# The first steps of a four-layer transformer kernel: extra TensorE products, whole-tile modulations, another order of small work on VectorE, ScalarE and GpSimd

## The chip, the cores and the metric

The kernel runs on one core of a Trainium2 chip. A core has TensorE for products (PE in the profile, and PEld for its weight loads), VectorE (DVE), ScalarE (ACT), GpSimd (POOL) and SyncE (SP), which here issues nearly all transfers. Each engine works through its own instructions in order, and semaphores make it wait for another. The metric is the time of one execution on the device, in microseconds. All data is float32.

## The reference

The input x has 128 sequences of 64 tokens with 128 channels. A condition of 128 vectors and a context of the same shape as x come with it. Four layers follow. The first one is what this case is about:

```python
mod = silu(t_emb) @ adaln_w + adaln_b
sh_sa, sc_sa, g_sa, sh_ff, sc_ff, g_ff = split(mod[:, None, :], 6)
xm = _ln(x) * (1.0 + sc_sa) + sh_sa
qkv = xm @ qkv_w + qkv_b                 # 16 heads of 8 channels
x = x + g_sa * (_attend(q, k, v) @ sa_proj_w + sa_proj_b)
x = x + _attend(_ln(x) @ q_w + q_b, context @ kv_w + kv_b) @ ca_proj_w + ca_proj_b
xm = _ln(x) * (1.0 + sc_ff) + sh_ff
x = x + g_ff * (gelu(xm @ fc1_w + fc1_b) @ fc2_w + fc2_b)
```

Layer 1 is one cross attention, layer 2 has the form of layer 0, and layer 3 is a mixture of three experts with a gate.

## The kernel before

The 8192 tokens are cut into 16 tiles of 512 tokens (8 sequences). A tile of x, `x[s]`, stays in SBUF for the whole program as four blocks of 128 tokens by 128 channels. Layer 0's self attention runs over the 16 tiles, then its cross attention, then its MLP, and so on through the layers.

For one tile of attention, `prepare` is a generator that is advanced piece by piece:

1. statistics: four `bn_stats` and four `bn_aggr` on DVE (L312, L314), then `rs`, the inverse standard deviation, on POOL (L321, L322);
2. `normed_by_pool`: `nmu` (L361) and four `xn` instructions (L364), on POOL, for the very first tile on DVE;
3. four transposes on PE into PSUM (`psT`, L334) and the modulation into `xm`: eight ACT instructions, one per sequence (L351), for the first tile eight on DVE (L349);
4. keys: the product `pk` (L428), the copy `kT` on ACT (L430), and four masked copies `kbd` (L436) on POOL, for the first tile on DVE;
5. queries: `pq` (L441) and `qT` on ACT (L443);
6. values: 32 small products `pvv` (L451) and two ACT copies into `vbd` (L456, L457). There are two `vbd` buffers, and each has to be cleared once by `clear` on POOL (L171 to L173) before its first use.

The attention itself advances in half steps of 256 tokens. `scores` does the score products `sc` (L470), the row maxima `mx` (L477) and the subtraction `e` (L479) on DVE. `turned` transposes `e` on PE (`pp`, L495) and takes exp on ACT (`eT`, L499), and `weighted` multiplies with the values (`po`, L512) and copies out on ACT (`o`, L520). There is only one PSUM buffer for `sc`, so the score products of a step wait for `e` of the step before. All the other products of a half step take turns in two PSUM buffers called `mm`.

In one half step `k` the order on the engines is written out by hand: scores of `k`, first half of the turning of `k-1`, values of `k-2`, a piece of some tile's preparation, the second half of the turning, more pieces of preparation. Before step 0 the pieces are advanced by calls of `ahead_1`; each number is the tile whose `prepare` goes one piece further. `condition` turns the condition and the bias vectors (`pc`, `pv`), and `first_mods` are three parts of the modulation vectors of layer 0 (`pm` on PE, L195, and two additions on DVE, L199). `first_tables` has five parts: the folded bias column (`pb`, L207), the gate table in two halves (`pg`, L224, the copy `gate_rows`, L225, and its transfer), and the folded bias row in two halves (L233, and `pb` with an addition, L237 and L238).

The order is final: the program runs under a manual schedule, and nothing moves instructions later.

Of the kernel before, what the change touches and what calls it, by code (L numbers as in the profile page):

```python
# [9 lines left out]
F32 = mybir.dt.float32  # L10
AF = mybir.ActivationFunctionType
ALU = mybir.AluOpType
# [3 lines left out]
P = 128  # L16
NST = 16
TT = 4
NB = 8
L = 64  # L20
# [39 lines left out]
def tile_kernel(ctx: ExitStack, tc: tile.TileContext, a: dict, out: bass.AP):  # L60
    nc = tc.nc
    V, S, G, T = nc.vector, nc.scalar, nc.gpsimd, nc.tensor
# [3 lines left out]
    def const(shape, name):  # L66
        return cp.tile(shape, F32, tag=name, name=name)
# [4 lines left out]
    out_d = out.rearrange("b n c -> (b n) c").rearrange("(s t p) c -> s p t c", t=TT, p=P)  # L72


    cond = const([P, P], "cond")
    nc.sync.dma_start(cond, a["cond_1024"])
    vec_rows = const([_NVEC, P], "vec_rows")
# [13 lines left out]
                nc.sync.dma_start(t, src.rearrange("(k p) n -> p k n", p=P))  # L91
                w[name] = t

    xs = [const([P, TT, P], f"x{s}") for s in range(NST)]

    def load_groups(which):
        for s in which:
            nc.sync.dma_start(xs[s], x_d[s])

    load_groups((0,))  # L100
    load_weights(("L0_xcond_adaln", "L0_xcond_qkv"))
    load_groups((1,))
    load_weights("L0_xcond_sa")
# [3 lines left out]
    for name, n in (("L0_xcond_ca_proj_b", P), ("L1_xcond_bp", P), ("L2_xcond_b_cproj", P), ("L3_xcond_router_b", 3)):  # L107
        t = const([P, n], name)
# [11 lines left out]
    make_identity(nc, ident)  # L120
    nhalf = const([P, TT], "nhalf")
    G.memset(nhalf, -0.5)

    stack, attention_stack = ExitStack(), ExitStack()
    dp = ctx.enter_context(tc.tile_pool(name="dp", bufs=1, space=bass.MemoryType.DRAM))
# [34 lines left out]

    def mm(name):
        return pools[1].tile([P, 512], F32, tag="mm", name=name)

# [4 lines left out]
    def clear(t):  # L170
        G.memset(t, 0.0)  # L171
        G.memset(t[0:L, :, :, 16:17], 1.0)
        G.memset(t[L:P, :, :, 17:18], 1.0)  # L173
# [4 lines left out]
    condT = const([P, P], "condT")  # L178
# [64 lines left out]
    def condition():  # L243
        pc = mm("pc")
        T.transpose(pc[:, :P], cond, ident)
        V.tensor_copy(condT, pc[:, :P])
        S.activation(scT, pc[:, :P], AF.Silu)
        pv = mm("pv")
        T.transpose(pv[:, :_NVEC], vec_rows, ident[:_NVEC, :_NVEC])
        V.tensor_copy(vec, pv[:, :_NVEC])  # L250
        V.tensor_scalar_add(vec1, vec, 1.0)
# [43 lines left out]
    def mod(name, i, s):  # L295

        return mods[name][:, i, ts(s, NB)].unsqueeze(2).broadcast_to([P, NB, L])

    def by_batch(t):
        return t.rearrange("p (b l) -> p b l", b=NB)  # L300
# [29 lines left out]
    def transposed(psum, src):  # L330

        ps = psum.tile([P, 512], F32, tag="mm", name="psT")
        for t in range(TT):
            T.transpose(ps[:, ts(t, P)], src[:, t, :], ident)  # L334
        return ps

    def modulated(pool, ps, name, scale, shift, s, tag="xm"):
        xm = pool.tile([P, NT], F32, tag=tag, name=tag)
        V.tensor_tensor(by_batch(xm), by_batch(ps), mod(name, scale, s), ALU.mult)
        G.tensor_tensor(by_batch(xm), by_batch(xm), mod(name, shift, s), ALU.add)  # L340
        return xm

    def modulated_by_batch(pool, ps, name, scale, shift, s, tag="xm", by_dve=False):
        xm = pool.tile([P, NT], F32, tag=tag, name=tag)
        for b in range(NB):
            k = NB * s + b
            m, p = (mods[name][:, i, k : k + 1] for i in (scale, shift))
            if by_dve:
                V.tensor_scalar(xm[:, ts(b, L)], ps[:, ts(b, L)], m, p, ALU.mult, ALU.add)  # L349
            else:  # L350
                S.activation(xm[:, ts(b, L)], ps[:, ts(b, L)], AF.Identity, bias=p, scale=m)  # L351
        return xm


# [2 lines left out]


    def normed_by_pool(pool, src, mv, rs, tag, engine=G):
        nmu = pool.tile([P, TT], F32, tag="nmu" + tag, name="nmu")  # L360
        G.tensor_scalar(nmu, mv[:, :, 0], -1.0, 0.0, ALU.mult, ALU.add)  # L361
        xn = pool.tile([P, TT, P], F32, tag=tag, name=tag)
        for t in range(TT):
            engine.tensor_scalar(  # L364
                xn[:, t, :], src[:, t, :], nmu[:, t : t + 1], rs[:, t : t + 1], ALU.add, ALU.mult
            )
        return xn
# [10 lines left out]
    def prepare(pools, at):  # L378

        pool, psum = pools[:2]  # L380
        s, layer = at["s"], at["layer"]
        eps = 1e-5 if layer == "L1c" else 1e-6
        cross = layer[2] == "c"
        if cross:
            c = pool.tile([P, TT, P], F32, tag="c", name="c", bufs=3)
            nc.sync.dma_start(c, ctx_d[s])
        yield
        if layer == "L1c":
            mv = x_mv[:, s]
            rs = inv_std(pool, mv, eps)  # L390
        else:
            mv, rs = stats_of(pool, xs[s], eps)
        yield
        xn = normed_by_pool(pool, xs[s], mv, rs, "xn", V if at.get("first") else G)
        if cross:
            cn = c
            if layer != "L0c":
                cn = pool.tile([P, TT, P], F32, tag="cn", name="cn", bufs=1)
                for t in range(TT):
                    rs, nb = (v[eps][:, s, t : t + 1] for v in (ctx_rs, ctx_nb))  # L400

                    if layer == "L1c" or s == 0:
                        G.tensor_scalar(cn[:, t, :], c[:, t, :], rs, nb, ALU.mult, ALU.add)
                    else:
                        S.activation(cn[:, t, :], c[:, t, :], AF.Identity, bias=nb, scale=rs)
        yield
        if layer == "L1c":
            kv_in = modulated_by_batch(pool, transposed(psum, cn), "L1_xcond_Wss_kv", 0, 1, s, "cm")
        elif cross:
            kv_in = copied(pool, transposed(psum, cn), "cm")  # L410
            if layer == "L0c":
                nc.sync.dma_start(ctxT[s], kv_in)
        else:
            q_in = kv_in = modulated_by_batch(
                pool, transposed(psum, xn), at["wmod"], 1, 0, s, by_dve=at.get("first", False)
            )
        yield
        if not cross:
            pass
        elif layer == "L1c":  # L420
            q_in = modulated(pool, transposed(psum, xn), "L1_xcond_Wss_q", 0, 1, s)
        else:
            q_in = copied(pool, transposed(psum, xn), "xm")
        yield


        pk = psum.tile([P, 512], F32, tag="mm", name="pk")
        T.matmul(pk, at["wk"], kv_in, start=True, stop=True)  # L428
        kT = pool.tile([P, NT], F32, tag="kT", name="kT")
        S.activation(kT, pk, AF.Identity, bias=at["bk"])  # L430
        i = turn[0] % 2
        turn[0] += 1
        vbd = vbds[i]
        kbd = pool.tile([P, 4, NB, L], F32, tag="kbd", name="kbd")
        for j in range(4):
            (V if at.get("first") else G).tensor_scalar(  # L436
                kbd[:, j], by_batch(kT), mask[:, j : j + 1], 1.0, ALU.mult, ALU.mult
            )
        yield
        pq = psum.tile([P, 512], F32, tag="mm", name="pq")  # L440
        T.matmul(pq, at["wq"], q_in, start=True, stop=True)  # L441
        qT = pool.tile([P, NT], F32, tag="qT", name="qT")
        S.activation(qT, pq, AF.Identity, bias=at["bq"])  # L443
        at.update(qT=qT, kbd=kbd)
        yield

        wv_pair = at["wv"].rearrange("p (i j d) -> p j i d", j=2, d=HD)
        pvv = psum.tile([P, NB, L], F32, tag="mm", name="pvv")
        for b in range(NB):
            for j in range(2):  # L450
                T.matmul(  # L451
                    pvv[ts(j, L), b, :], kv_in[:, ts(b, L)], wv_pair[:, j],
                    start=True, stop=True,
                )
        pv4 = pvv.rearrange("p b (i d) -> p b i d", d=HD)
        S.copy(vbd[0:L, :, :, 0:HD], pv4[0:L])  # L456
        S.copy(vbd[L:P, :, :, HD : 2 * HD], pv4[L:P])  # L457
        at["vbd"] = vbd
# [713 lines left out]

    def stages():
        ats = [attention_of(s, layer) for layer in ("L0s", "L0c") for s in groups]
        ats[0]["first"] = True
        ahead_1, steps_1 = attend(pools, ats)
        ahead_2, steps_2 = attend(
            pools, [attention_of(s, layer) for layer in ("L1c", "L2s", "L2c") for s in groups]
# [33 lines left out]
            return turns[last - 1 :]  # L1212


        clear(vbds[0])
        ahead_1(0, 1, 2, 3)
        condition()
        ahead_1(0, 0)
        first_mods[0]()
        ahead_1(0, 0, 1, 2, 0, 0, 1)  # L1220
        psum_for_attention()

        steps_1[0]([lambda: ahead_1(2), lambda: clear(vbds[1]), lambda: ahead_1(1, 1, 0, 3)])
        tables = first_tables()
        steps_1[1]()
        first_mods[1]()
        steps_1[2]()
        for f in tables[:3]:
            f()
        steps_1[3]((), tables[3:])  # L1230
        for f in steps_1[4:6]:
            f()
        first_mods[2]()
        n = last + 2 + len(heads_0)
        for f in steps_1[6:-n]:
            f()
        rest = into_mlp(steps_1, heads_0, turns_0)
        second = [(0, 1, 2), (0,), (1, 0), (0, 0, 1, 2), (0, 1, 1, 2, 0, 0, 3, 3)]
        n_ = len(second)
# [66 lines left out]
```

## Time and profile before

| | |
|---|---|
| median of 3 runs | 1635.25 us (1635.12 to 1635.38) |
| the profiled execution | 1632.74 us |
| its span, first to last instruction | 1631.0 us |
| PE busy | 1577.1 us, 97% |
| DVE busy | 1296.5 us, 79% |
| ACT busy | 1037.2 us, 64% |
| POOL busy | 1084.7 us, 67% |

The busy time is that of one profiled execution. A matmul's end is modelled, so a PE that is busy is not a PE at its peak. One float32 product of `pk` shows as two PE rows. Times in the text such as "at 20.45" are microseconds from the first instruction of the span.

### The profile page before, as it was taken

How to read it: one execution, taken by the hardware profiler on the slowest of the kernel's cores; microseconds unless marked ns; L12 is line 12 of the kernel's file. 1: busy time of each engine (PE TensorE's matmuls, PEld its weight loads, DVE VectorE, ACT ScalarE, POOL GpSimd, SP SyncE). 2: the span in 40 equal slices, each digit the busy share in tenths (PEclk: the TensorE clock that was granted, in tenths of full speed). 3: DMA queues.
4: the chain of work that ended last, by engine and by line, in shares of the span. 5: the costliest groups of instructions: out<-in, count | busy, mean ns of one | idle time of the engine just before them, and what ended most of it. 6: DMA issues, size and time to landing. Idle time of an engine off the chain costs nothing.

```text
span 1631.0 us, 64964 instructions
## 1 busy us (share of the span) xinstructions
PE 1577.1 (97%) x27842; PEld 1089.0 (67%) x27842; DVE 1296.5 (79%) x2430; ACT 1037.2 (64%) x1710; POOL 1084.7 (67%) x1818
## 2 busy tenths in 40 slices
PE   6999999998999899999999999998999999999998
PEld 4677777776554477777777677776777666666665
DVE  7999999998576688899999999997454576666666
ACT  5788777776333587788888888886334544444443
POOL 6688776776799888986778876665876333333322
PEclk9999999999999999999999999999999999999999
DMA  7334443322202022211333532222433111111100
GB/s 208 82 82 97 108 121 91 89 80 62 61 27 59 27 58 62 63 47 49 85 94 82 116 95 63 73 57 57 120 91 78 30 39 37 40 33 35 34 11 20
DMA packets 146783, 112.71 MB, mean 69 GB/s; under 512 B 36357, under 2 KB 125247, under 8 KB 146495
## 3 DMA queue, kind: packets, MB, share of 16 engines
q1 hardware_dynamic: 146288, 108.53, 25.8%
q8 instruction: 219, 3.59, 1.0%
q14 instruction: 69, 0.57, 0.1%
q10 hardware_dynamic: 207, 0.03, 0.0%
HBM read 83.99 MB, written 14.02 MB: 60 GB/s over the span
## 4 chain that ended last, share of the span: by engine, by line
PE 79%; DVE 13%; ACT 3%; POOL 3%; issue 1%; DMA 0%; SPq 0%; POOLq 0%; DVEq 0%; ACTq 0%
PE sc L470 10%; PE pp L495 9%; PE po L512 7%; PE ph L1063 6%; PE ph L1064 6%; DVE e L479 6%; DVE mx L477 6%; PE ph L676 6%; PE po L1094 5%; PE psT L334 5%; PE pk L428 5%; PE py L555 4%; PE py L692 3%; PE pvv L451 3%; PE pq L441 3%; PE py L682 2%
## 5 line engine op out<-in xcount | busy, mean ns | idle before, releaser
L499 ACT ACTIVATE eT<-pp 128x1024 f32<-128x1024 f32 x320 | 329.8, 1030 | 159.4 <-PE pp L495 159.3
L477 DVE TENSOR_REDUCE mx<-sc 128x32 f32<-128x2048 f32 x160 | 366.6, 2291 | 58.6 <-PE sc L470 58.6
L479 DVE TENSOR_TENSOR e<-sc,mx 128x2048 f32<-128x2048 f32 x160 | 366.6, 2291 | 5.4
L495 PEld LDWEIGHTS pp<-ident,e 64*128 64x128 f32 x5120 | 184.9, 139 | 140.7 <-ACT eT L499 44.8
L495 PE MATMUL pp<-ident,e 64*128 64x64 f32 x5120 | 228.7, 229 | 7.1 <-DVE e L479 4.7
L364 POOL TENSOR_SCALAR xn<-x,nmu,rs 128x128 f32<-128x128 f32 x508 | 224.7, 456 | 13.3
L436 POOL TENSOR_SCALAR kbd<-kT,mask 128x512 f32<-128x512 f32 x316 | 213.2, 693 | 26.9 <-ACT kT L430 24.5
L549 POOL TENSOR_TENSOR oT<-o,rb 128x512 f32<-128x512 f32 x80 | 102.3, 1278 | 164.5 <-DMA rb<-recs 63.6
L470 PE MATMUL sc<-kbd,qT 32*64 32x256 f32 x5120 | 180.5, 389 | 16.4 <-DVE e L479 15.4
L677 ACT ACTIVATE h<-ph,vec 128x512 f32<-128x512 f32 x128 | 87.4, 688 | 154.8 <-PE ph L676 154.6
L512 PE MATMUL po<-eT,vbd 128*32 128x64 f32 x10240 | 178.4, 221 | 1.1 <-issue 1.0
L1070 ACT ACTIVATE h<-h 128x512 f32<-128x512 f32 x112 | 70.6, 630 | 148.1 <-DVE h L1066 129.2
L512 PEld LDWEIGHTS po<-eT,vbd 128*32 128x32 f32 x10240 | 151.9, 110 | 14.0 <-issue 1.6
L322 POOL TENSOR_TENSOR rs<-rs,nhalf 128x4 f32<-128x4 f32 x128 | 130.4, 1019 | 10.7
L470 PEld LDWEIGHTS sc<-kbd,qT 32*64 32x64 f32 x5120 | 98.1, 131 | 53.1 <-issue 20.2
L1066 DVE TENSOR_TENSOR h<-ph,ab 128x512 f32<-128x512 f32 x112 | 77.0, 688 | 56.2 <-PE ph L1064 56.1
L312 DVE BATCH_NORM_STATS2 st<-x 128x6 f32<-128x128 f32 x512 | 110.5, 278 | 0.8 <-DMA x<-in_x_dram 0.3
L1099 DVE SCALAR_TENSOR_TENSOR acc<-po,pr,acc 128x128 f32<-128x128 f32 x192 | 67.3, 350 | 44.1 <-PE po L1094 39.5
L1063 PE MATMUL ph<-nx,w 128*128 128x512 f32 x192 | 99.9, 602 | 0.0
L520 ACT COPY o<-po 128x512 f32<-128x512 f32 x160 | 95.8, 598 | 5.2 <-PE po L512 3.6
L1064 PE MATMUL ph<-u,w_ev 128*128 128x512 f32 x192 | 98.0, 592 | 0.0
L1094 PEld LDWEIGHTS po<-w_2o,h 128*128 128x128 f32 x768 | 92.1, 192 | 8.7 <-issue 8.4
(261 smaller groups left out, 2849.8 us busy)
## 6 DMA issues: line engine op xcount, KB each, us to landing
rb<-recs SPq DMA_DIRECT2D x80, 256.0 KB
c<-in_ctx_dram SPq DMA_DIRECT2D x64, 256.0 KB
o<-o SPq DMA_DIRECT2D x320, 32.0 KB
gt<-gate_L_xcond_sa_proj_w SPq DMA_DIRECT2D x32, 256.0 KB
gt<-gate_L_xcond_W_proj SPq DMA_DIRECT2D x32, 256.0 KB
gt<-gate_L_xcond_W_mlp SPq DMA_DIRECT2D x32, 256.0 KB
x<-in_x_dram SPq DMA_DIRECT2D x16, 256.0 KB
ctxT<-cm SPq DMA_DIRECT2D x16, 256.0 KB
```

Of the source, the lines that this page charges most:

```text
L322: G.tensor_tensor(rs, rs, nhalf, ALU.pow)
L364: engine.tensor_scalar(xn[:, t, :], src[:, t, :], nmu[:, t : t + 1], rs[:, t : t + 1], ALU.add, ALU.mult)
L436: (V if at.get("first") else G).tensor_scalar(kbd[:, j], by_batch(kT), mask[:, j : j + 1], 1.0, ALU.mult, ALU.mult)
L470: T.matmul(sc[ts(h, L), g, ts(t2, 256)], qT[ts(g, 32), ts(b, L)], kbd[ts(g, 32), :, b, :], start=True, stop=True,)
L477: V.tensor_reduce(mx, sc.rearrange("p g (m k) -> p (g m) k", k=L), AX.X, ALU.max)
L479: V.tensor_tensor(e, sc.rearrange("p g (m k) -> p (g m) k", k=L), mx.unsqueeze(2).broadcast_to([P, 32, L]), ALU.subtract,)
L495: T.transpose(pp[:, h, ts(4 * g2 + 2 * i + t2, L)], e6[ts(h, L), 2 * gg + g2, t2, i], ident[ts(h, L), ts(h, L)],)
L499: S.activation(eT[:, gg], pp, AF.Exp, scale=HD ** -0.5)
L512: T.matmul(po[ts(g, 32), i, ts(2 * t2 + h, L)], at["vbd"][:, 4 * u + 2 * t2 + h, 2 * g + i, :], e7[:, g // 2, h, g % 2, i, t2, :], start=T ...
L1063: T.matmul(ps, wn, d["nx"], start=True, stop=False)
L1064: T.matmul(ps, we, d["u"], start=False, stop=True)
L1094: T.matmul(po[:, ex, :], d[q][:, ts(t, P)], k3["w_2o"][:, q, :], start=r == 0, stop=r == 1)
```

## The change

All edits concern the first steps.

- A tile `busy` of ones is written by DVE, and `keep_busy(n)` issues n products of it with itself into an `mm` buffer. Nothing reads them. Six stand at the very start of PE's order, three after the first modulation vectors, five after the transposes of tile 0.
- The load of `x[0]` is issued ahead of that of the condition.
- In `condition` the copy `condT` moves from DVE to ACT, behind `scT`, and a small Exp on ACT follows it.
- DVE does the statistics of tile 0 before it copies the bias vectors, and the first modulation vectors before `xn`. `xn` of tile 0 subtracts the mean directly, without `nmu`.
- The modulation of tile 0 is a multiplication and an addition on DVE over the whole 512 tokens. That of tile 2 is a multiplication on DVE and an addition on POOL. Tile 1 and tiles from 3 on stay with eight ACT instructions.
- `clear(vbds[0])` moves behind POOL's work for tile 0's statistics. `clear(vbds[1])` moves behind step 0, which on POOL is behind `kbd` of tile 1, the addition for tile 2 and `xn` of tile 3. DVE's statistics of tile 2 move behind `kbd` of tile 0.
- The second part of the modulation vectors moves from after step 1 to after step 2, and the last part of the tables, the folded row, from step 3 to step 7.

```diff
+    load_groups((0,))
     cond = const([P, P], "cond")
     nc.sync.dma_start(cond, a["cond_1024"])
...
-    load_groups((0,))
     load_weights(("L0_xcond_adaln", "L0_xcond_qkv"))
...
+    taken = const([P, TT], "taken")
+    busy = const([P, P], "busy")
+    V.memset(busy, 1.0)
...
+    def keep_busy(n):
+
+        p = mm("pi")
+        for _ in range(n):
+            T.matmul(p[:, 0:P], busy, busy, start=True, stop=True)
...
-        V.tensor_copy(condT, pc[:, :P])
         S.activation(scT, pc[:, :P], AF.Silu)
+        S.copy(condT, pc[:, :P])
+
+        S.activation(taken, nhalf, AF.Exp)
...
-    def modulated(pool, ps, name, scale, shift, s, tag="xm"):
+    def modulated(pool, ps, name, scale, shift, s, tag="xm", engine=G):
         xm = pool.tile([P, NT], F32, tag=tag, name=tag)
         V.tensor_tensor(by_batch(xm), by_batch(ps), mod(name, scale, s), ALU.mult)
-        G.tensor_tensor(by_batch(xm), by_batch(xm), mod(name, shift, s), ALU.add)
+        engine.tensor_tensor(by_batch(xm), by_batch(xm), mod(name, shift, s), ALU.add)
         return xm
...
     def normed_by_pool(pool, src, mv, rs, tag, engine=G):
+        if engine is V:
+            xn = pool.tile([P, TT, P], F32, tag=tag, name=tag)
+            for t in range(TT):
+                V.tensor_scalar(
+                    xn[:, t, :], src[:, t, :], mv[:, t, 0:1], rs[:, t : t + 1],
+                    ALU.subtract, ALU.mult,
+                )
+            return xn
...
-            q_in = kv_in = modulated_by_batch(
-                pool, transposed(psum, xn), at["wmod"], 1, 0, s, by_dve=at.get("first", False)
-            )
+            first = at.get("first", False)
+            if first or at.get("third", False):
+                q_in = kv_in = modulated(
+                    pool, transposed(psum, xn), at["wmod"], 1, 0, s, engine=V if first else G
+                )
+            else:
+                q_in = kv_in = modulated_by_batch(pool, transposed(psum, xn), at["wmod"], 1, 0, s)
...
-        ats[0]["first"] = True
+        ats[0]["first"] = ats[2]["third"] = True
...
+        keep_busy(6)
+        ahead_1(0, 1, 2, 3, 0)
+        condition()
+        first_mods[0]()
+        keep_busy(3)
+        ahead_1(0)
         clear(vbds[0])
-        ahead_1(0, 1, 2, 3)
-        condition()
-        ahead_1(0, 0)
-        first_mods[0]()
-        ahead_1(0, 0, 1, 2, 0, 0, 1)
+        ahead_1(0)
+        keep_busy(5)
+
+        ahead_1(0, 1, 0, 0, 2, 1)
         psum_for_attention()
 
-        steps_1[0]([lambda: ahead_1(2), lambda: clear(vbds[1]), lambda: ahead_1(1, 1, 0, 3)])
+        steps_1[0]([lambda: ahead_1(2, 1, 1, 0, 3)])
+        clear(vbds[1])
         tables = first_tables()
         steps_1[1]()
+        steps_1[2]()
         first_mods[1]()
-        steps_1[2]()
         for f in tables[:3]:
             f()
-        steps_1[3]((), tables[3:])
+        steps_1[3]((), tables[3:4])
         for f in steps_1[4:6]:
             f()
         first_mods[2]()
         n = last + 2 + len(heads_0)
-        for f in steps_1[6:-n]:
-            f()
+        for k, f in enumerate(steps_1[6:-n]):
+            f((), tables[4:] if k == 1 else ())
```

More of the change, by code (lines that the diff above doesn't have):

```diff
@@ L72, in tile_kernel, with load_groups @@
     out_d = out.rearrange("b n c -> (b n) c").rearrange("(s t p) c -> s p t c", t=TT, p=P)
+    xs = [const([P, TT, P], f"x{s}") for s in range(NST)]
+    def load_groups(which):
+        for s in which:
+            nc.sync.dma_start(xs[s], x_d[s])
+    load_groups((0,))
     cond = const([P, P], "cond")
@@ L92, in load_weights @@
                 w[name] = t
[L94 to L98, printed above, removed]
-    load_groups((0,))
     load_weights(("L0_xcond_adaln", "L0_xcond_qkv"))
@@ L335, in transposed, with modulated_by_batch @@
         return ps
-    def modulated(pool, ps, name, scale, shift, s, tag="xm"):
+    def modulated(pool, ps, name, scale, shift, s, tag="xm", engine=G):
         xm = pool.tile([P, NT], F32, tag=tag, name=tag)
         V.tensor_tensor(by_batch(xm), by_batch(ps), mod(name, scale, s), ALU.mult)
-        G.tensor_tensor(by_batch(xm), by_batch(xm), mod(name, shift, s), ALU.add)
+        engine.tensor_tensor(by_batch(xm), by_batch(xm), mod(name, shift, s), ALU.add)
         return xm
-    def modulated_by_batch(pool, ps, name, scale, shift, s, tag="xm", by_dve=False):
+    def modulated_by_batch(pool, ps, name, scale, shift, s, tag="xm"):
         xm = pool.tile([P, NT], F32, tag=tag, name=tag)
@@ L347, in modulated_by_batch @@
             m, p = (mods[name][:, i, k : k + 1] for i in (scale, shift))
[L348 to L351, printed above, removed]
+            S.activation(xm[:, ts(b, L)], ps[:, ts(b, L)], AF.Identity, bias=p, scale=m)
         return xm
     def normed_by_pool(pool, src, mv, rs, tag, engine=G):
+        if engine is V:
[6 more added lines that the diff above has]
+            return xn
         nmu = pool.tile([P, TT], F32, tag="nmu" + tag, name="nmu")
@@ L363, in normed_by_pool @@
         for t in range(TT):
-            engine.tensor_scalar(
+            G.tensor_scalar(
                 xn[:, t, :], src[:, t, :], nmu[:, t : t + 1], rs[:, t : t + 1], ALU.add, ALU.mult
```

## The prediction

> **What bounds the kernel now.** I read the page's busy rows first, then the table of windows over the first 40 us, then the chain of waits and the timeline there, since every edit lies in the first eight half steps.
>
> ```profile
> PE   6999999998999899999999999998999999999998
> DVE  7999999998576688899999999997454576666666
> 10.00:15.00 5.00, 3.61 (x4) 1.17 (x4) 4.21 (x25) 0.69 (x1) 2.29 (x4) 1.00 0.85 159
> 15.00:20.00 5.00, 2.95 (x68) 2.15 (x68) 3.60 (x5) 2.76 (x9) 4.80 (x12) 1.00 1.21 298
> 25.00:30.00 5.00, 2.92 (x52) 2.74 (x52) 3.97 (x10) 4.29 (x6) 4.73 (x11) 0.83 0.84 255
> 30.00:35.00 5.00, 5.00 (x124) 3.01 (x124) 3.35 (x4) 2.18 (x4) 0.45 (x1) 0.83 0.68 186
> ```
>
> PE is full in nearly every slice but the first (40.8 us, digit 6). The columns of a window are PE, PEld, DVE, ACT, POOL, clock: PE stands still some 2 of 5 us at 15 to 20 and at 25 to 30, and the clock is 0.83 over two stretches, that is half rate for about 3.4 us in all. So the change can win only a few us of 1631.
>
> ```profile
> 9.21 2.12 DVE xm L349 x8
> 11.37 2.09 PE pk L428 x2
> 14.20 1.68 DVE kbd L436 x4
> 17.93 1.11 ACT xm L351 x4
> 24.71 1.28 ACT L499
> 29.21 1.15 PE pm L195 x4
> 30.37 1.83 PE sc L470 x32
> 63.07 2.30 DVE mx L477
> 65.40 2.30 DVE e L479
> ```
>
> The chain passes from one engine to the next until about 40 us, then it settles: sc, mx, e, sc. I call S0, S1, ... the start of the score products (sc) of each half step. The timeline gives 16.02, 22.10, 30.30, 36.90, 43.78, 49.80, 55.95, 61.84, 67.83, 73.77, 79.76. The settled step is 5.97 us (73.77 less 61.84, halved): 1.2 until mx may start, 2.30 mx, 2.30 e, 0.15 to the next sc. Nothing after S0 can go below that, so the whole prize is the shift of S10. The steps of 8.20 (S1 to S2), 6.60 and 6.88 hold 3.8 us of slack; the head holds the rest.
>
> ```profile
> 11.37 2.07 PE L428 MATMUL pk<-xm,L_xcond_qkv_w 128*128 128x512 f32 x2 [2.27 <-DVE xm L349]
> 13.83 0.19 POOL L321 TENSOR_SCALAR rs<-mv 128x4 f32<-128x4 f32 x1
> 15.64 1.87 POOL L364 TENSOR_SCALAR xn<-x,nmu,rs 128x128 f32<-128x128 f32 x4
> 19.45 1.81 POOL L171 MEMSET vbd<- 128x2048 f32 x1
> 20.45 1.12 PE L428 MATMUL pk<-xm,L_xcond_qkv_w 128*128 128x512 f32 x2 [1.49 <-ACT xm L351]
> 29.32 0.58 ACT L456 COPY vbd<-pvv 64x512 f32<-64x512 f32 x1 [0.46 <-PE pvv L451]
> ```
>
> pk takes 2.07 at 11.37 and 1.12 at 20.45: PE is at half rate before its first load (the clock column says 1.00 there, so I go by durations). POOL's rs, xn and memset will matter below.
>
> **The head, S0.** Moving x0 ahead of cond shifts x0 0.45 earlier on SP's queue (stats at 4.15, not 4.60) and cond behind 256 KB. Bounds for cond: 3.5 (its present reach to pc at 3.10, plus one issue) to 4.3 (behind all of x0). I take 4.3; it costs nothing, because pm waits for the adaln weights until 5.71 with the same bytes ahead of them; scT is ready by 5.1 (if cond landed after 4.9, the head would move with it). The fourteen products have no row. Nearest is pm: 1.19 for two products cold, 0.71 at 55.30 warm, so six take 2.1 to 3.6 us from about 1.0 and end by 4.6, under that same wait; three and five take 1.1 to 3.0 in gaps of about 1.2. With a warm clock that is free, and I take warm: PE is busy nearly all of 1.0 to 6.5. condT and the early Exp load (1.28) go to ACT, idle until kT; clear(vbd0), about 2.4 us with its small memsets, sits on POOL in the wait for tile 1's stats: both nothing.
>
> Then: pm 5.7 to 6.4, mods 0.60 to 7.05, xn 1.11 to 8.2 (no nmu, and mods no longer after it), psT to 8.5, xm in two DVE tensor_tensors. Their row is y<-py,gt 128x512 at 0.63 (62.16), so 1.26 in place of 2.11: 9.85. pk 1.06, 0.13 to ACT, kT 0.69, kbd 1.67: 13.5. S0 is 13.6, **2.4 earlier**.
>
> **S1, where it is lost again.** DVE now does tile 2's stats after kbd, but POOL's order still has rs of tile 2 before nmu and xn of tile 1. Stats end at 13.5 + 1.15 = 14.65. In the trace rs started at 13.83 and S1 came 8.27 later through xn, psT, ACT's eight modulations (2.48), pk, psT. All of those stand as they were, so S1 = 14.7 + 8.27 = 23.0, **0.9 later** than before; e of step 0 is done at 19.4 and waits for nobody.
>
> **S2.** Gone: ACT's 2.48 for tile 2 (now 0.63 on DVE inside the sc of step 1, plus an add on POOL), the Exp load, pm (1.22) ahead of S2. With pp, pq, pvv done by S1 + 4.7 the step is DVE's 5.97: 28.95, **1.35 earlier**.
>
> **S3, a new wait.** clear(vbd1) was at 19.45 in idle POOL time. It now stands behind kbd 2.70, the new xm add (1.26, the row of POOL's 128x512 x<-x,gt) and nmu and xn 2.05. From S1 + 0.15 the memset ends at about 31.1. ACT's vbd copies of tile 1 wait for it, and behind them on ACT: eT (free to go at 30.7, goes at 32.3), o, kT; behind those on PE pk, pp, psT, pm, pb. From 32.3: eT 1.02, o 0.59, kT 0.65, then pm 0.7, mods 0.60, pb: S3 = 36.3, **0.6 earlier** only.
>
> **S4 to S10.** pb of the row table (the gap at 43.36 before S4) has left this step: 42.2, 1.55 earlier. gate_rows 0.42 and stats 1.15 now both fall between e and mx: 6.3 for this step, where the trace has 6.02. S5 to S7 go as before, within 0.15. pb (0.25 on PE) and its add (0.29 on DVE) land in step 7, which has 0.3 idle on PE: 0.3 lost. S10 is **0.85 earlier** at full clock. The gate table's DMA leaves 0.5 sooner, the SP queue keeps its order otherwise.
>
> **The clock rule against the trace.** sc in S0 ends at 14.7 and psT of tile 1 comes at 17.0: PE idles 2.3 us. In the trace PE idled 24.86 to 27.07 (2.2 us) and the two 0.83 windows follow, with sc 1.80 in place of 1.12 and pm 1.22 for 0.71. The Trainium skill, "TensorE: Matmul & The Clock Gate", Part 1, wants about 3.4 us of idleness in a free-running window, and its closing table warns only of gaps above 3 us; it gives this gap a price of 0 and the sum -0.85. By the trace a gap of 2.2 us is enough. Price from 0 (half rate over before pk at 21.2) to 1.9 (psT tails 0.3, pk 0.95 and sc 0.68 all slow). I take 0.3: the half-rate stretch of the trace lasted 3.4 us, and from the end of a window near 18 it would be over at about 21.5.
>
> Sum: -0.85 + 0.3 = -0.55. The profiled execution took 1632.74 (span 1631.0 and 1.74 around it), so 1632.2; the runs' median is 2.5 us above it, and I carry that over: 1634.7.
>
> **The rivals.**
> 1. The head start carries to the end. If tile 1 is ready in time (S1 = S0 + 6.08 as before), S1 is 19.7, and S3 and all that follows 3.3 earlier: -4.1, 1631.2. For it: S0 itself is solid. Against: POOL's order, which needs tile 2's stats first.
> 2. Slower, by the clock in the new gap at 14.7. It decides when PE's idle share of a window exceeds what the trace shows to be enough (about 2.2 of 3.4 us); if half rate then lasts past 21.2, the full 1.9 is paid at S1 and S2: +1.05, 1636.3. For it: 2.3 us of idleness. Against: the window must lie right.
> 3. The products do not lift the clock in time. Then pm, psT, pk stay at half rate and the five products delay pk: S0 about 15.2, and S1 moves with kbd: +0.75, 1636.0. Against: PE is busy over any window between 1.0 and 7.8.
>
> **How the numbers follow.** A change of 0.2% (3.3 us) is about what a measurement of this kernel can tell from none. Likeliest case 0.62, own range 1633.6 to 1635.6; rival 1: 0.10, of which 0.08 beyond 0.2%; rival 2: 0.18, rival 3: 0.10, together 0.05 beyond. Range 1632.6 to 1636.9: it leaves out rival 1 and the far ends of the others.
>
> **What would show it.** Right: pk about 1.1 from 9.9; S0 near 13.6; psT of tile 1 not before 16.5; S1 near 23; ACT standing before the vbd copies at 27.7 to 31.1; S10 near 79. Wrong: S1 below 21 (rival 1), clock under 1.00 in 15 to 25 with pk near 2.0 (rival 2), pk above 1.8 (rival 3).

## The result, and the profile after

The changed kernel takes 1637.01 us (median of 22 runs, 1634.81 to 1642.73) beside 1635.14 us for the kernel before on the same chip: ratio 1.0016, 95% interval 1.0010 to 1.0023. Predicted was 1634.7, a little faster; it is a little slower, 0.1 us beyond the upper end of the predicted range, on the side of rival 2. The profiled execution took 1634.81 us (span 1633.0) against 1632.74 (1631.0): 2.0 us more of span, of which 1.7 are there at S10.

The busy rows of the page after: slice 1 of PE is fuller, by the products that nothing reads and by work at half rate; no other digit of PE differs, and none of DVE by more than one tenth.

```profile
PE   7999999998999899999999999998999999999998
DVE  6999999999566688899999999998454576666666
```

The table of windows of the changed kernel (PE, PEld, DVE, ACT, POOL, clock, DMA share, GB/s):

```profile
10.00:15.00 5.00, 3.26 (x15) 1.79 (x13) 4.01 (x14) 1.38 (x2) 1.22 (x2) 1.00 0.89 179
15.00:20.00 5.00, 2.79 (x36) 1.42 (x36) 4.66 (x11) 0.00 (x0) 3.45 (x9) 0.71 1.19 303
20.00:25.00 5.00, 4.34 (x38) 2.95 (x38) 2.15 (x9) 3.72 (x11) 2.79 (x6) 0.50 1.15 287
25.00:30.00 5.00, 4.94 (x72) 2.63 (x72) 3.03 (x3) 2.18 (x3) 4.32 (x8) 0.77 0.90 266
30.00:35.00 5.00, 3.66 (x144) 3.09 (x144) 4.70 (x10) 2.93 (x4) 4.66 (x8) 1.00 0.74 207
```

The clock is 0.71, 0.50 and 0.77 from 15 to 30, where before it was 0.83 twice, later. Its record in the trace gives half rate from 17.1 for 10.2 us; before it was 3.4 us, from 28.3. PE looks busier at 20 to 30 than at 15 to 20, but that is half-rate work. ACT does nothing at all between 15 and 20: it waits for tile 1.

The chain of waits of the changed kernel, in order of time:

```profile
1.76 4.49 DMA L_xcond_adaln_w<-in_L_xcond_adaln_w_dram
6.38 1.19 PE pm L204 x4
...
11.58 1.11 PE pk L448 x2
...
13.44 1.67 DVE kbd L456 x4
15.11 0.78 DVE st L323 x4
15.89 0.29 DVE mv L325 x4
16.26 0.19 POOL rs L332
16.54 1.01 POOL rs L333
17.54 0.18 POOL nmu L377
17.82 0.46 POOL xn L380
18.33 1.78 PE psT L345 x4
...
22.67 2.08 PE pk L448 x2
...
25.60 2.00 PE sc L490 x32
...
38.22 0.53 DVE mod_L_xcond_adaln_w L208 x2
38.79 0.38 PE pb L216 x2
39.17 1.05 PE sc L490 x32
```

From kbd of tile 0 the chain goes through tile 2's statistics (st, mv, rs) before it comes to nmu and xn of tile 1, whose own statistics had been done since 12.5. That is the wait that the prediction named. pk of tile 0 takes 1.11 (2.07 before): the products do lift the clock. pk of tile 1 takes 2.08 (1.12 before): it is lost again just after. And the head begins with the adaln weights, which the chain of before did not show.

The timeline of the changed kernel gives the two waits of PE and ACT that matter later; the last entry is the idle time and who ended it.

```profile
18.33 1.77 PE L345 MATMUL psT<-ident,xn 128*128 128x128 f32 x4 [1.95 <-POOL xn L380]
31.21 1.81 POOL L180 MEMSET vbd<- 128x2048 f32 x1
33.06 0.58 ACT L476 COPY vbd<-pvv 64x512 f32<-64x512 f32 x1 [2.03 <-POOL vbd L180]
```

The starts of the score products, by the timeline of each profiled execution, with the stretches of half rate before 100 us:

| | S0 | S1 | S2 | S3 | S4 | S10 | half rate (start, length) |
|---|---|---|---|---|---|---|---|
| before | 16.02 | 22.10 | 30.30 | 36.90 | 43.78 | 79.76 | 28.3, 3.4 |
| predicted | 13.6 | 23.0 | 28.95 | 36.3 | 42.2 | 78.9 | 0.3 us of loss allowed |
| after | 15.26 | 25.53 | 32.38 | 39.10 | 45.09 | 81.43 | 17.1, 10.2 |

### The profile page after: what moved, and what is told of

Its sections match the earlier page's. It is cut to its first block, busy times and chain, and to the rows that moved or that the text cites. A ratio compares the mean times of both kernels' runs of the same rounds, so it can differ in the third digit from the quotient of the medians.

```text
span 1633.0 us, 65008 instructions
## 1 busy us (share of the span) xinstructions
PE 1583.3 (97%) x27870; PEld 1094.4 (67%) x27870; DVE 1296.0 (79%) x2425; ACT 1035.4 (63%) x1704; POOL 1083.8 (66%) x1818
## 4 chain that ended last, share of the span: by engine, by line
PE 78%; DVE 12%; POOL 3%; ACT 3%; DMA 2%; issue 1%; SPq 0%; POOLq 0%; DVEq 0%; ACTq 0%
PE sc L490 9%; PE pp L515 9%; PE po L532 7%; PE ph L1083 6%; PE ph L1084 6%; DVE mx L497 5%; PE ph L696 5%; DVE e L499 5%; PE po L1114 5%; PE psT L345 5%; PE pk L448 4%; PE py L575 4%; PE py L712 3%; PE pq L461 3%; PE pvv L471 3%; PE py L702 2%
```

## The experiments

Each was timed beside the kernel before on its own chip, six runs or more; ratios have 95% intervals. Where nothing else is said the edit is made to the changed kernel. One sum of all starts is at the end of this section.

**The kernel before against itself.** No edit.

> The kernel before once more. Its own first half steps are sampled in another phase of the clock's windows. If the profile of before lay in a slow phase (half rate at 28.3 to 31.7), S10 here is 0.3 to 1.3 earlier than 79.8 when that stretch is absent; if it was a common one, S10 is within 0.3. The time is that of before within its interval, which shows what the comparison can tell apart.

Ratio 0.9999 (0.9990 to 1.0007). S0 16.11, S1 23.38, S2 30.72, S10 79.47: S1 differs by 1.3 us between two executions of one program, S10 by 0.3. So differences of 0.001 in time, and of 0.3 us at S10, are the floor below; a single S1 or S2 can be off by more than 1 us where the clock differs.

**PE kept busy in the gap before tile 1.** Ten more products that nothing reads, between the score products of step 0 and the transposes of tile 1.

```diff
-        steps_1[0]([lambda: ahead_1(2, 1, 1, 0, 3)])
+        steps_1[0]([lambda: keep_busy(10), lambda: ahead_1(2, 1, 1, 0, 3)])
```

> Ten more products that nothing reads stand between the score products of step 0 and the transposes of tile 1, where PE idled 2.0 us; no other order changes. Theory A, the clock falls because of that gap: PE keeps the full clock through 17 to 25 us, psT, pk and sc of tile 1 take 0.6 to 0.7, 1.1 and 1.1 in place of 1.8, 2.1 and 2.0, S1 comes 9.3 after S0 (10.3 in the changed kernel), S2 by 30.6, and the time falls by 1.3 to 1.9 us. Theory B, tile 1 is late only by POOL's order: S1 stays near S0 + 9.3 and the time falls by less than 0.5.

Ratio 1.0011 (1.0002 to 1.0021). The windows and the timeline of this run:

```profile
15.00:20.00 5.00, 4.16 (x55) 3.33 (x55) 4.66 (x12) 0.00 (x0) 3.12 (x8) 1.00 1.20 299
20.00:25.00 5.00, 3.46 (x55) 2.23 (x63) 2.88 (x10) 4.19 (x11) 3.21 (x9) 1.00 1.09 285
```

```profile
22.95 1.13 PE L448 MATMUL pk<-xm,L_xcond_qkv_w 128*128 128x512 f32 x2 [1.48 <-ACT xm L359]
24.60 1.12 PE L490 MATMUL sc<-kbd,qT 32*64 32x256 f32 x32
```

The clock stays at 1.00, pk takes 1.13 and sc 1.12. S0 to S2 takes 14.89 (30.59 less 15.70) and 17.12 in the changed kernel (32.38 less 15.26): **the half rate costs 2.23 us.** What is left of S0 to S1, 8.90, is the order alone: the prediction's 9.4 for it was right within half a microsecond, and the kernel before needed 6.08. In time, 1.3 to 1.9 us were expected; 1.0011 beside 1.0016 is 0.8 us, and within the floor.

**nmu and xn of tile 1 ahead of rs of tile 2 on POOL.**

```diff
-        ahead_1(0, 1, 0, 0, 2, 1)
+        ahead_1(0, 1, 0, 0, 1, 2)
```

> POOL does nmu and xn of tile 1 ahead of rs of tile 2 (two numbers of the ahead list swapped). If POOL's order makes tile 1 late: xn of tile 1 starts by 14.5, PE has no gap after the score products of step 0, S1 comes 6.1 to 7.3 after S0 (10.3 in the changed kernel). The clear of the second vbd buffer still stands behind xn of tile 3, so S3 keeps a wait and S10 gains only about 1 to 2 us. If the clock alone is the cause, the gap is gone here too and S1 gains no more than in the fill experiment (about 1.3).

Ratio 1.0013 (1.0002 to 1.0023). S1 21.27, S2 27.43: the first wait is gone, 5.0 us by S2. But S3 is 37.20. The timeline and a window of this run:

```profile
31.02 0.58 ACT L476 COPY vbd<-pvv 64x512 f32<-64x512 f32 x1 [5.10 <-POOL vbd L180]
...
32.29 1.10 PE L448 MATMUL pk<-xm,L_xcond_qkv_w 128*128 128x512 f32 x2 [2.07 <-POOL rs L332]
```

```profile
35.00:40.00 5.00, 4.30 (x55) 2.92 (x54) 1.98 (x6) 2.69 (x9) 4.02 (x9) 0.50 0.02 5
```

With tile 1 early, clear(vbd1), still behind kbd, the addition and xn on POOL, comes too late: ACT stands for 5.10, PE behind it for 2.07, and half rate follows (33.8 to 40.7). The row of pk names POOL's rs, which was done at 31.77; pk starts 0.1 after the second copy out of pvv (31.61 and 0.58), so it is the buffer that it waited for. S2 to S3 takes 9.77. Taking away one wait has only bared the next.

**clear(vbd1) back in front of kbd of tile 1.**

```diff
-        steps_1[0]([lambda: ahead_1(2, 1, 1, 0, 3)])
-        clear(vbds[1])
+        steps_1[0]([lambda: ahead_1(2), lambda: clear(vbds[1]), lambda: ahead_1(1, 1, 0, 3)])
```

> The clear of the second vbd buffer goes back to where it stood, between xn of tile 2 and rs of tile 3; the rest is as changed. If the vbd copies' wait for it is a cost of its own: ACT no longer stands 2.0 us before them, S2 to S3 shrinks from 6.7 to about 6.6 at half clock before, or from 7.4 to 6.6 at full clock, and S10 gains 0 to 0.8. Since tile 1 is late in any case, S1 stays at S0 + 9.3 or more, and the time stays within 1 us of the changed kernel.

Ratio 1.0028 (1.0017 to 1.0040). S1 26.18, S2 32.21, S3 38.92: S2 to S3 is 6.71 where the changed kernel has 6.72. While tile 1 is late, nobody waits long enough for the clear to move a step; by itself this edit gains nothing.

**Both.**

> Both reorderings together. The sum of rows says S0 15.3, S1 21.5 to 22.7, S2 27.6 to 29.3, S3 34.3 to 35.9, S10 76.8 to 78.4, which is 1.4 to 3 us ahead of the kernel before (79.8) and 3 to 4.6 ahead of the changed one (81.4). If the loss had another cause than these two waits, S10 stays above 80.

Ratio 0.9992 (0.9983 to 1.0002). S0 15.44, S1 21.41, S2 27.57, S3 34.29, S10 76.53, no half rate in the first steps. The timeline of this run:

```profile
16.49 0.71 PE L345 MATMUL psT<-ident,xn 128*128 128x128 f32 x4
20.16 1.81 POOL L180 MEMSET vbd<- 128x2048 f32 x1
...
26.19 0.58 ACT L476 COPY vbd<-pvv 64x512 f32<-64x512 f32 x1
```

psT follows sc at once, the clear, with its two small memsets, is over at 22.46, 3.7 before the copy that needs it, and neither has a wait behind it. S10 is 4.9 us ahead of the changed kernel; the two waits and the clock that fell with them are more than its whole loss at S10 (1.67).

**Without the fourteen products.** The three calls of `keep_busy` and the memset of `busy` removed.

> The changed kernel without the fourteen products that nothing reads. If they earn what they were priced at: pm, psT and pk stay at half rate, pk takes 2.07, S0 comes at 15.8 to 16.2 in place of 15.26 (the products also delay psT by 0.4 and pk by 0.1, which is given back). The late tile 1 stays, S1 is S0 + 10 or so, and the time is 0 to 1 us above the changed kernel. If the products themselves delay the chain more than the clock brings, S0 is below 15.26.

Ratio 1.0025 (1.0016 to 1.0034), an interval that overlaps that of the change. S0 16.32, 1.06 later than with them; 0.39 of that is there at pm already (6.77 against 6.38), as the weights landed later, so the products are worth about 0.7 here. The timeline of this run has pk of tile 0 back at half rate:

```profile
11.67 2.07 PE L447 MATMUL pk<-xm,L_xcond_qkv_w 128*128 128x512 f32 x2 [1.51 <-DVE xm L350]
```

**Only the fourteen products, in the kernel before.** Six first, three after the first modulation vectors, five after the transposes of tile 0; all else as before.

> The kernel before with nothing added but the fourteen products that nothing reads, at the places where the change puts them. If the products lift the clock by themselves: pk of tile 0 near 1.1 instead of 2.07, S0 about 1 us earlier (15.0), S1 near 21.1, S10 near 78.7, ratio about 0.9995. If the changed kernels share a loss of 1 to 2 us that the products bring (buffers turned by one, the clock's phase later on), S10 is earlier and the ratio is nevertheless 1.0003 or more.

Ratio 1.0002 (0.9991 to 1.0013), no difference. pk takes 1.10, but S0 is 15.49, a gain of 0.53 only: the three products, still cold (at half rate), lie in front of psT, and xm starts at 9.59 (9.21 before). S1 is 22.45, S10 78.55, 1.2 earlier. Both halves of the first expectation, 15.0 and 21.1, were too early, and the time shows nothing of S10's gain.

**The order of the loads as before.** x0 behind the condition and the bias vectors again.

> The changed kernel with the condition's load ahead of x0 again. In the changed kernel pm waited for the adaln weights until 6.38, before it was 5.71. If the order of the two loads does that: pm at 5.7, S0 0.5 to 0.7 earlier than 15.26, cond read by 3.2. If it is chance of the transfers, pm stays at 6.2 or later. S1 and the rest move with S0; the time is 0 to 0.7 below the changed kernel.

Ratio 1.0028 (1.0018 to 1.0037). I had expected S0 earlier, and it is 16.74, later by 1.5. The timeline of this run:

```profile
6.05 0.68 PE L204 MATMUL pm<-scT,L_xcond_adaln_w 128*128 128x128 f32 x4 [1.59 <-DVE vec L261]
...
7.20 1.80 POOL L180 MEMSET vbd<- 128x2048 f32 x1
7.30 2.37 DVE L371 TENSOR_SCALAR xn<-x,mv,rs 128x128 f32<-128x128 f32 x4
```

The adaln weights are no longer the last to come, as I had expected, but pm now waits for DVE's copy of the bias vectors, which the change had put behind x0's statistics, and xn runs beside POOL's memset and takes 2.37 in place of 1.10: the first two of its four instructions, begun at 7.30 and 7.55, end at 9.09 and 9.15, just after the memset (9.01), the other two take 0.33 each. Even so xm ends only 0.3 later than in the changed kernel; the rest of the 1.5 is the clock, at half rate from 8.3 to 15.1 (and again from 18.5). Load order, DVE's order and the place of the clear belong together: in S0, undoing the load order alone is worse than keeping all three, by 1.5 here and by 1.0 in the next two runs (16.16 against 15.13). In time the intervals overlap.

**Both repairs, the load order as before, and the second modulation vectors in front of step 2.**

```diff
         steps_1[1]()
-        steps_1[2]()
         first_mods[1]()
+        steps_1[2]()
```

> Both reorderings (xn of tile 1 ahead of rs of tile 2, the second clear back in POOL's idle time), the condition's load first, and the second part of the modulation vectors back ahead of step 2. By the rows: S0 14.7 to 15.3, S1 6.0 later, S2 to S3 6.0 to 6.4 in place of 6.7, S10 75.5 to 76.5, which is 0 to 1 us ahead of the kernel with both reorderings and 3 to 4 ahead of the kernel before. If the loss left over is not in the first steps, it is not faster than that kernel.

Ratio 1.0000 (0.9990 to 1.0011). S0 16.16, S2 28.30, S3 34.27, S10 76.51: the step from S2 to S3 is 5.97, the settled length, where the run with both repairs has 6.72. The load order gave that gain away in the head, with S0 0.7 later.

**Both repairs and the second modulation vectors in front of step 2, the changed load order kept.**

> The changed kernel with tile 1's mean and rs put ahead of tile 2's on POOL, clear(vbd1) put back in front of POOL's kbd of tile 1, and the second modulation vectors put back in front of step 2; the load order stays as changed. If the two waits are the whole cause and the later modulation vectors cost 0.7 us between S2 and S3: S0 15.4, S1 21.4, S2 27.6, S3 33.6, S10 75.8, ratio to the kernel before about 0.9985. If their place is worth nothing: S3 34.3, S10 76.5, ratio 0.9992 as without this edit.

Ratio 0.9991 (0.9980 to 1.0001). S0 15.13, S2 27.27, S3 33.25, S10 75.49, as expected within 0.4. The chain of this run shows the modulation additions behind the statistics and ahead of mx. There sc runs until 28.39 anyway, so they hold mx by 0.3 at most:

```profile
27.90 0.28 DVE mv L325 x4
28.18 0.49 DVE mod_L_xcond_adaln_w L208 x2
28.67 2.21 DVE mx L497
...
30.90 2.30 DVE e L499
...
33.25 1.12 PE sc L490 x32
```

In the changed kernel they came after e (38.22), with pb behind them (38.79), and sc could not start before both. That, and not the clear, is what kept its S2 to S3 at 6.72.

**As the run before, with the last part of the tables back in step 3.**

```diff
-        steps_1[3]((), tables[3:4])
+        steps_1[3]((), tables[3:])
...
-            f((), tables[4:] if k == 1 else ())
+            f()
```

> As the run with all three repairs, but with the last part of the tables put back from step 7 to step 3. If moving it out of step 3 was worth something: S4 0.5 to 1.5 later, S7 to S8 0.2 shorter, S10 76.2 to 77, ratio 0.0003 to 0.0006 above that run. If it only moved work from one full step to another: S10 75.8 as there, ratio the same.

Ratio 0.9983 (0.9973 to 0.9992), the lowest of all, though the versions around it overlap with it; it is faster than the kernel before and than the changed one. S3 to S4 is 6.88 instead of 5.98, and the chain of this run shows why:

```profile
38.98 0.44 DVE gate_rows L234
...
39.46 0.50 PE pb L246 x2
...
39.99 0.29 DVE L_xcond_ca_proj_b L247
```

S4 to S10 is 35.97 instead of 36.26. Spreading the tables thus gains 0.90 in step 3 and loses 0.29 later, which is the prediction's 0.95 (in its S4) and 0.3. In time this 0.6 cannot be seen: 0.9983 beside 0.9991, intervals overlapping.

**As the run with all three repairs, with tile 2 modulated by ACT.**

> As the run with all three repairs, but with tile 2 modulated by ACT's eight instructions as in the kernel before. If ACT's eight (2.5 us) stood on the path to S2: S2 28.5 to 30 in place of 27.6, S10 1 to 2 later, ratio 0.0006 to 0.001 above that run. If ACT had room for them under step 1: S2 27.6 and S10 75.8 unchanged.

Ratio 0.9984 (0.9973 to 0.9996). The timeline of this run:

```profile
21.20 2.48 ACT L359 ACTIVATE xm<-psT,mod_L_xcond_adaln_w 128x64 f32<-128x64 f32 x8
...
27.09 1.12 PE L490 MATMUL sc<-kbd,qT 32*64 32x256 f32 x32
```

S1 to S2 is 5.99, S10 75.31. ACT's eight instructions had room under step 1 once tile 1 came in time. The whole-tile modulation of tile 2 gains nothing.

**Both of these together.**

> The three repairs with both further edits taken back: the last part of the tables in step 3, and tile 2 modulated by ACT. If each is worth 0 to 1 us by itself and they do not meet: S0 15, S4 39.8, S10 75.6 to 76, ratio 0.9975 to 0.9985. If neither matters: 0.9985 to 0.9992, as with the three repairs alone.

Ratio 0.9987 (0.9977 to 0.9997). S0 14.82, S4 39.65, S10 75.64: at the steps as expected, in time no better than either alone.

**The kernel before with two unused tiles reserved.**

> The kernel before with the two new constant tiles reserved and no new instruction, so that all later tiles lie 528 bytes further on. If the loss of 1 to 3 us that the changed kernels show after S10 comes from where the tiles lie: S0 to S10 as before (79.5 to 79.8) and a ratio of 1.001 or more. If it comes from something else (which of the later pauses of PE fall into half rate): ratio 0.9993 to 1.0007.

Ratio 1.0002 (0.9993 to 1.0012), S10 79.75. That the later tiles lie 528 bytes further on makes no difference that can be seen.

The starts, half-rate stretches before 100 us and ratios of the main runs:

| | S0 | S1 | S2 | S3 | S10 | half rate | ratio |
|---|---|---|---|---|---|---|---|
| before | 16.02 | 22.10 | 30.30 | 36.90 | 79.76 | 28.3, 3.4 | 1 |
| after | 15.26 | 25.53 | 32.38 | 39.10 | 81.43 | 17.1, 10.2 | 1.0016 |
| gap filled | 15.70 | 24.60 | 30.59 | 37.44 | 79.68 | none | 1.0011 |
| tile 1 first | 15.29 | 21.27 | 27.43 | 37.20 | 80.93 | 33.8, 6.8 | 1.0013 |
| clear first | 15.92 | 26.18 | 32.21 | 38.92 | 81.15 | 19.5, 6.8 | 1.0028 |
| both repairs | 15.44 | 21.41 | 27.57 | 34.29 | 76.53 | none | 0.9992 |
| no products | 16.32 | 26.58 | 32.71 | 39.43 | 81.80 | cold to 26.9 | 1.0025 |
| load order back | 16.74 | 27.01 | 33.84 | 40.56 | 82.79 | 8.3, 6.8; 18.5, 10.2 | 1.0028 |
| three repairs | 15.13 | 21.05 | 27.27 | 33.25 | 75.49 | 8.3, 3.4 | 0.9991 |
| three, tables back | 14.88 | 20.80 | 27.02 | 33.00 | 75.85 | 7.7, 3.4 | 0.9983 |

## Why the prediction was wrong

**The clock price was mis-sized.** "I take 0.3" for half rate in the new gap; it measured 2.23, beyond even the upper bound of 1.9. It was no chance of one execution: the two other runs with the same late tile 1 and a warm clock fell to half rate too (clear first, load order back), and their S0 to S2, 16.29 and 17.10, lies 1.40 and 2.21 above the 14.89 of the filled gap. The mechanism, rival 2, was stated with its threshold, and the idle time was counted too small: the prediction looked only at the 2.3 us after sc of step 0. PE also stands before it, from the end of pq at 13.54 to S0 at 15.26, waiting for kbd (1.72). In the clock record every stretch but the last is a multiple of 3.41 us long. So I count windows of that length: here they begin at 10.3, 13.7, 17.1 and so on, and the one from 13.7 holds 1.60 of the first wait and 0.70 of the second: PE busy 33% of it. And the length was taken from the one stretch of before, 3.4 us, which lasted one window because PE had no pause in it. Here PE stood 1.25 us of the window from 17.1 and 0.66 of that from 20.5, and half rate lasted three windows.

The rule of the Trainium skill that the prediction weighed here ("TensorE: Matmul & The Clock Gate", Part 1: about 3.4 us of idleness in a free-running window) would have made this price 0. The trace decides against its size of the gap, not against the free-running window: no wait here was longer than 1.95 us, and two of them, together 2.3 us of one window, were enough.

**The head was mis-sized.** S0 was to be 13.6 and is 15.26. (a) "pm waits for the adaln weights until 5.71 with the same bytes ahead of them": pm starts at 6.38, at 6.77 in the run without the products and at 6.47 in the one with three repairs. The bytes ahead were the same, their order was not. In the second run of before it starts at 5.81:

```profile
5.81 1.19 PE L195 MATMUL pm<-scT,L_xcond_adaln_w 128*128 128x128 f32 x4 [1.96 <-DVE mv L314]
```

The row names DVE's mv, which pm does not read; by the DMA's semaphore in the trace the weights had landed at 5.67, and at 6.25 in the changed kernel. (b) "With a warm clock that is free", because "PE is busy nearly all of 1.0 to 6.5": PE stood 1.48 us before pm, so the window from 3.4 to 6.8 was only 50% busy, and full rate was granted from 10.3 on. So pm took 1.19, not 0.7, and the three products, cold, lay in front of psT. psT ended at 10.03, 0.8 after xn, where 0.3 was taken. Rival 3 came true for pm and psT, though not for pk. (c) xm took 0.69 twice, 0.1 more than the two times 0.63 of the row that I used. Together 0.67, 0.5, 0.5 and 0.1, less 0.1 that xn gave back: the 1.66.

How cold this head is depends on where the windows lie: in five of the runs with the products (load order back, and the four with three repairs and the changed load order) full rate was granted from 4.1 to 4.9 and pm took 0.68, but all five fell back at 7.5 to 8.3. In none of the sixteen executions is S0 below 14.82.

The head also had a term at nothing that was not: clear(vbd0) "in the wait for tile 1's stats". In the changed kernel it cost little by luck, as xn began at 8.14 and the memset was over at 8.16. At the predicted 7.05 xn would have stood beside it and, as in the run with the load order back, where it ended 0.66 after the memset, have ended at about 8.8 in place of 8.2 (an estimate from that run).

**S1, the lost head start, was right.** Rival 1 was right to be discounted: POOL's order makes tile 1 wait for tile 2, S0 to S1 is 8.90 at full clock against 9.4 predicted, and turning the order round brings 5.97.

**S3, the new wait, was right in mechanism and wrong in place.** As S2 came 3.4 later than predicted, the clear at 31.21 hardly held anything (the wait of 2.03 on ACT lay beside e and sc). It bites where S2 is early, at 9.77 in the run with tile 1 first. What stood between e and S3 was the modulation additions and pb, which the prediction had as part of the same delay.

**The sum at S10.** Against the predicted 79.2 (with its 0.3 for the clock) the profile has 81.43, 2.2 later: head +1.66, S0 to S1 +0.87, S1 to S2 +0.90, S2 to S3 -0.63, the rest -0.28, less the 0.3 already allowed. From S0 to S2 the surplus of 1.77 is the 2.23 of the clock less what the order took below its estimate. The median lies 2.3 above the prediction.

**What stays open.** S10 is followed only loosely by the time. Both repairs put S10 3.2 earlier and bring 0.0008 (1.3 us); filling the gap puts it where before had it and is 0.0011 slower (1.8 us). On the average the edited kernels lie nearly 2 us above what their S10 says. It is not the products (the run without them has the same surplus), nor the place of the tiles, as far as it was moved. Later pauses of PE, near 404, 1131 and 1282 us, are followed by half rate in some executions and not in others, as the windows happen to lie (at 1282 the window was 41% busy in the second run of before, which went to half rate, and 54% in the changed kernel, which did not), and a profiled execution of one program differs from its median by up to 4.7 us (1628.33 beside 1633.02 in the run called "both of these together", whose mean clock there was 0.998). The one at 1282 costs 1.7 us: the eight profiled executions that have it lose that much against the first of before between 1243 and 1582 us, the seven others 0.02 at most. Whether such pauses make up the surplus was not settled.

## What to carry to other kernels

Price a pause of PE by the whole window that it falls in: add every wait of PE within about 3.4 us, also the ones that were there before, and expect the half rate to last until a window is almost full of work. When early work is reordered, write each in-order queue down with its due times: here a POOL instruction for tile 2 stood in front of one for tile 1, and a memset in front of nobody until the first fault was mended. Undo parts in pairs, not only one by one: two waits in a row each hide the other, and either repair alone (1.0013, 1.0028) says that it is worthless, where both give 0.9992 and, with the third, 0.9983 to 0.9991.

## What the runs showed of the hardware

- **A threshold for the clock.** I cut the sixteen profiled executions into windows of 3.41 us, counted from each change in the clock record, and took PE's busy share of each from its rows in the trace. At full clock, every window with less than 43% was followed by half rate, none with more than 58% was, and between them it went either way. In the first 70 us the two kinds part at 46% (ten windows, 33% to 46%, then half rate) and 48%. From half rate, windows of 82% and more led back to full, those of 81% and less did not; one of 94% (clear first, from 19.5) is an exception, and so is one of 88% in the run without the products (from 20.1, before its record's first entry). So the same pause of 2.16 us in step 1, at 24.9 in before, brings half rate when one window holds it (37% busy) and none when two share it: the second run of before, the one with only the products and the one with two unused tiles have it too, and stay at full rate.
- **An instruction of DVE or POOL can stand until the other engine's is over.** The four xn of tile 0 on DVE take 1.10 alone, 1.85 and 2.37 beside POOL's memset of 128x2048, and the two that stand end within 0.15 us of the memset's end (load order back: 9.09 and 9.15, memset 9.01). Four xn on POOL take 1.74 alone and 2.17 to 2.50 beside DVE's kbd, and the first of them carries the loss: in the run with three repairs it takes 1.19 in place of 0.45, from 13.95 to 15.14, with the last kbd over at 14.98. The one that was running keeps its length: 1.80 for the memset, 1.67 for kbd. The prediction costed both as if alone.
- **The order of issue moves a landing.** With x0 in front of the 64 KB of the condition, the adaln weights behind both land at 6.22 to 6.63 in ten executions, and pm starts 0.13 later. With the condition in front they land at 5.58 to 5.96 in six, four of the kernel before and its variants and two of the changed one with the load order back. Why is not shown.
